# Token tiles side by side, the second attention's loads in order of use, and routing weights by powers of e on GpSimd

## The chip, the cores and the metric

The kernel runs on one core of one Trainium2 chip. The metric is the device time of one execution in microseconds (us), the median of several runs. The core has five engines that matter here: TensorE (PE in the profile) multiplies matrices, VectorE (DVE), ScalarE (ACT) and GpSimd (POOL) work on rows of 128 partitions, and SyncE (SP) does little but issue DMAs. Each runs its own list of instructions in order. SBUF is the memory on the core from which they work, PSUM the one that TensorE writes to.

## The reference, cut to what matters

The input is two images of 56 x 56 positions with 256 channels, all float32. Each image passes through a group norm and a neighbourhood attention ("Attention" below) with a residual. Then all 6272 positions, now called tokens, pass through two more layers:

```python
# x: (2, 256, 56, 56)
x = x + _L0_conv_ref(_gn(x), ...)        # 1x1 and 3x3 convolutions to q, k, v; 7x7 neighbourhoods,
                                         # dilation 1 and 2, softmax with a position bias; projection
t = _to_tokens(x)                        # (2, 3136, 256)
t = t + _L1_attn_ref(_ln_t(t), ...)      # linear attention, elu + 1, then a two-layer perceptron
t = t + _L1_ffn_ref(_ln_t(t), ...)       # 8 experts, two for each token
x = _from_tokens(t, x)

# inside _L1_ffn_ref
probs = softmax(xt @ Wr + br)
top_p, top_idx = top_k(probs, 2)
weights = top_p / top_p.sum(axis=-1, keepdims=True)
h = gelu(xe @ W1 + b1, approximate=False)     # for each expert: 256 -> 1024
y = h @ W2 + b2                               #                 1024 -> 256
out = sum over the two chosen experts of weights * y
```

The two weights of a token follow from its two largest logits m0 and m1 alone: with d = exp(m1 - m0) they are 1 / (1 + d) and d / (1 + d). That is what the kernel computes.

## The kernel before, in words

The program treats the first image's convolution and Attention, then the linear attention of the first image ("half 0"), then the second image's Attention, then the linear attention of the second image ("half 1"), and the experts wherever tokens are ready.

The linear attention works on groups of four tiles of 128 tokens, 14 groups in all. Groups 0 to 5 are in half 0, and groups 6 to 13 in half 1, of which the last three have two, two and one tile. The router's work for a group stands in `route`:

- `stats` and `norm` make normalised rows of the tokens, in a tile `row` whose columns hold the 256 channels, the token's number, the two weights and a flag.
- `top_two` finds the two largest logits and their experts, on VectorE.
- `weights` takes m1 - m0 (L2013), its Exp on ScalarE (L2014), and the two quotients on VectorE (L2015 to L2019; `rsum` is the first of these).
- `chosen` and `before` count, for each expert, the tokens up to here (L2056; `cnt` carries the count on to the next group). Two small matmuls (L2060, L2061) make places in the expert's list of them. VectorE turns those into integers `si`, through `sf` (L2063 to L2069).
- Eight indirect DMAs, issued by GpSimd, send the rows to their places in `xs` in DRAM. They are made by the helper `scatter` (L167), one for each of the four tiles and two experts.

A token's perceptron precedes this. Its matmuls are L1939 (with a Relu on ScalarE, L1942) and L1955, four blocks of which share three PSUM buffers (`ps_h`). VectorE frees each with `u` (L1962). The norm of the message takes squares on ScalarE (L1784) and a power of -1/2 on GpSimd (L260); `dt`, `z` and `qz` on VectorE (L1872, L1878, L1864) divide the linear attention by its denominator.

The experts work on tiles of 256 of an expert's tokens. For each, `fetch` issues on SyncE a DMA of the rows `xr` (L1521) and of the weights `w1e` and `w2e` (L1525, L1529); `turn` transposes the rows on TensorE (`px`, L1554), scales them to `xe` on VectorE and loads `b2e` (L1562). Then come the matmuls of L1585 with Gelu on ScalarE (L1589), those of L1603, the weighting on VectorE (L1609) and an indirect DMA that adds the result to the output (L167, `y`). The first 14 tiles run beside the second Attention and half 1; the rest, from tile 14 on, run alone afterwards. Beside the first of these the table for the last tiles is made from the final counts (matmul L1372, VectorE L1374), and `fill` pads the experts' lists.

Four things set the order of the work around the change.

- TensorE's order is written out by hand (`manual_schedule`, with strings of letters as turns). The other engines' instructions are placed by a scheduler that follows the order of the program, priorities (`high_priority`) and hints: `issue_after(x)` puts an instruction behind `x`.
- `newest` holds the last copy on VectorE ([0]) and the last power on GpSimd ([1]), to be named in such hints.
- Tiles of SBUF come from pools that open and close. A tile may lie over bytes of an older one, and its first writer then waits for the older one's last reader, even if that is a DMA. The pools of half 0 and half 1 have one-letter names: `sm` (small tiles, `p3s`) and `lp` (`p3l`) are two of them. `Tokens.place` lays out a half's tokens `t_00` to `t_05` (or `t_10` on) and, after them, their transposes `xT_00` to `xT_05`. The second Attention's pools open after half 0's close, so its first tiles lie over those.
- In the second Attention, `band0(r)` is the work of a band of eight image rows. Its tables of position bias are loaded by `fetch(s, r)` (L704, eight DMAs for one of s = 0), and the tokens' q and k by `prepare(g)` (`ld`, two DMAs, L789; transposed at L757). `v0` is loaded at L844. The scores are exponentiated (L647) and multiplied by the table (`p`, L648).

Of the kernel before, what the change touches and what calls it, by code (L numbers as in the profile page):

```python
# [13 lines left out]
F32 = mybir.dt.float32  # L14
AF = mybir.ActivationFunctionType
ALU = mybir.AluOpType
# [4 lines left out]
P = 128  # L21
# [24 lines left out]
E = 8  # L46
# [79 lines left out]
def hybrid_kernel(ctx: ExitStack, tc: tile.TileContext, a: dict, out: bass.AP):  # L126
# [5 lines left out]
    make_identity(nc, ident)  # L132
    mhalf = const.tile([P, 4], F32, name="mhalf")
    nc.vector.memset(mhalf, -0.5)


    td = dram.tile([B * T, C], F32, name="td")
# [20 lines left out]
    def apart(ins, mine, others, reason="rows of their own"):  # L158

        for group in others:  # L160
            tc.declare_no_dep(ins, group=group, reason=reason)
        for group in mine:
            tc.add_to_no_dep_group(group, ins)

    def scatter(dst, index, src, mine, others, **kw):

        ins = nc.gpsimd.indirect_dma_start(  # L167
            out=dst[:, :], out_offset=bass.IndirectOffsetOnAxis(ap=index, axis=0),
            in_=src, in_offset=None, **kw,
        )  # L170
        apart(ins.ins, mine, others)

    evac_n = [0]

    newest = [None, None]

    def evac(dst, src):

# [12 lines left out]
    class Tokens:  # L191
# [14 lines left out]
        def place(self, half, pool, late):  # L206

            pools = [pool] * (NH6 - 1) + [late]
            self.t[half] = [p.tile([P, 4, C], F32, name=f"t_{half}{i}", bufs=1) for i, p in enumerate(pools)]
            self.xT[half] = [  # L210
                p.tile([P, 2, 4 * P], F32, name=f"xT_{half}{i}", bufs=1) for i, p in enumerate(pools)
            ]

        def at(self, n0, n):

# [382 lines left out]
    class Attention:  # L598
# [115 lines left out]
        def run(self):  # L714
# [121 lines left out]
            def band0(r):  # L836
                yield blocks(8 * r + 16)
                if banks is not None and r == 0:
                    for k in range(2):
                        self.ahead[0, k] = self.fetch(0, k)  # L840
                yield from prepared(r + 1, 1)
                v0 = vp.tile([TT, 4, P], F32, name="v0")
                for c in range(4):
                    nc.sync.dma_start(  # L844
                        v0[:, c, :],
                        yimg[8 * r : 8 * r + 8, c * KC : (c + 1) * KC, 2 * C : 2 * C + P],
                    )
                i0, i1 = max(0, 8 * r - 3), min(HH, 8 * r + 11)
                ni = i1 - i0
                sums = [None]  # L850

                def chunk(hf, c):
                    j0, j1 = max(0, KC * c - 3), min(WW, KC * c + 17)
                    q = qT0[:, i0:i1, j0:j1]
                    got = []

                    def first():
                        got.append(self.scores(
                            TT, [(kT0[r][:, c].rearrange("p r c -> p (r c)"), q, 0)],
                            self.table(0, (r > 0) + (r == NG - 1), (c > 0) + (c == 3)), j1 - j0,  # L860
                        ))

                    def rest():
                        if c == 2 * hf:
                            po = self.ps_o.tile([P, 2, 512], F32, name="po")
                            sums[0] = po[:, :, : ni * 31].rearrange("p k (i j) -> p k i j", j=31)
                        h0 = (0, 25)[hf]
                        sub = sums[0][:, :, :, j0 - h0 : j1 - h0]
                        self.values(
                            TT, got[0], [(None, q, 0, v0[:, c, :], sub[:, 0], sub[:, 1])], c == 2 * hf  # L870
                        )

                    return first, rest

                def done(hf):
                    h0 = (0, 25)[hf]
                    for j, a0, a1 in ((r, i0, 8 * r + 4), (r + 1, 8 * r + 4, i1)):
                        o = 8 * j - 4
                        accumulate(
                            strip0(j)[:, :, a0 - o : a1 - o, h0 : h0 + 31], sums[0][:, :, a0 - i0 : a1 - i0, :]  # L880
                        )
                    if hf == 0:
                        return
                    for j in (r, r + 1) if r == NG - 1 else (r,):
                        a0, a1 = max(0, 8 * j - 4), min(HH, 8 * j + 4)
                        self.normalise(
                            strips0.pop(j)[:, :, a0 - 8 * j + 4 : a1 - 8 * j + 4, :].rearrange("p k r c -> p k (r c)"),
                            o0[:, a0:a1, :].rearrange("p r c -> p (r c)"), (a1 - a0) * WW,
                        )

                for hf in range(2):
                    for c in (2 * hf, 2 * hf + 1):
                        yield from step(*chunk(hf, c), (lambda hf=hf: done(hf)) if c % 2 else lambda: None)
# [731 lines left out]
    def linear(ph, tk, half, behind=None):  # L1625
# [286 lines left out]
        def feed_forward(n0, n, m2T, out):  # L1912
# [3 lines left out]
            for oc in range(4):  # L1916
                if oc == 0:
                    pa = ps_a.tile([P, 512], F32, name="pa", tag="a")
                    for ct in range(2):
                        for k in range(n):  # L1920
                            nc.tensor.matmul(
                                pa[32 * k : 32 * k + 32, :P], wr[:, ct, :], xT[:, ct, k * P : (k + 1) * P],
                                start=(ct == 0), stop=(ct == 1), skip_group_check=True,
                            )
                    la = lp.tile([P, P], F32, name="la", bufs=1)
                    evac(la[: 32 * n, :], pa[: 32 * n, :P])
                if oc == 2:
                    pl = ps_a.tile([P, 4, 32], F32, name="pl", tag="a")
                    nc.tensor.transpose(
                        pl.rearrange("p k e -> p (k e)")[:, : 32 * n], la[: 32 * n, :], ident[: 32 * n, : 32 * n]  # L1930
                    )
                    up = sm.tile([P, 4], F32, name="up1")[:, :n]
                    nc.vector.tensor_scalar(up, tk.up[:, n0 : n0 + n], 1.0, None, ALU.add)
                    lg = sm.tile([P, 4, E], F32, name="lg")
                    nc.vector.tensor_tensor(lg[:, :n], pl[:, :n, :E], bc(up, E), ALU.mult)
                p1 = ps_h.tile([P, 512], F32, name="p1", tag="h")
                for k in range(4):
                    rhs = xT[:, k, :] if k < 2 else m2T[:, k - 2, :w]
                    nc.tensor.matmul(  # L1939
                        p1[:, :w], fw1[:, k, oc * P : (oc + 1) * P], rhs, start=(k == 0), stop=(k == 3)  # L1940
                    )
                nc.scalar.activation(hT[:, oc, :w], p1[:, :w], AF.Relu, bias=hb[:, oc : oc + 1])  # L1942
                yield
# [66 lines left out]
        def weights(rt, ms, row, n):  # L2010

            r = rt.sm.tile([P, 4], F32, name="rsum")[:, :n]
            nc.vector.tensor_tensor(ms[1], ms[1], ms[0], ALU.subtract)  # L2013
            nc.scalar.activation(ms[1], ms[1], AF.Exp)  # L2014
            nc.vector.tensor_scalar(r, ms[1], 1.0, None, ALU.add)  # L2015
            nc.vector.reciprocal(r, r)
            nc.vector.tensor_tensor(row[:, :n, C + 1], ms[1], r, ALU.mult)
            nc.vector.tensor_scalar(ms[0], ms[1], -1.0, 1.0, ALU.mult, ALU.add)
            nc.vector.tensor_tensor(row[:, :n, C + 2], ms[0], r, ALU.mult)  # L2019

        def route(n0, n, logits):
# [32 lines left out]
            for k in range(n):  # L2054
                nxt = before[:, k + 1, :] if k < n - 1 else cnt
                nc.vector.tensor_tensor(nxt, before[:, k, :], m[:, k, :], ALU.add)  # L2056
            weights(rt, ms, row, n)
            yield
            pp = ns.bank()[:, : 4 * E].rearrange("p (k e) -> p k e", e=E)
            nc.tensor.matmul(pp[:, :n], rt.tri, m[:, :n], start=True, stop=False)  # L2060
# [4 lines left out]
            for k in range(K):  # L2065
                sf = sm.tile([P, 4], F32, name=f"sf{k}")[:, :n]
                nc.vector.tensor_tensor(ohs[k], ohs[k], slot, ALU.mult)
                nc.vector.tensor_reduce(sf, ohs[k], AX.X, ALU.add)
                nc.vector.tensor_copy(si[:, k, :n], sf)  # L2069
            store(n0, n)  # L2070
            late = [f"xlate{run}"] if (n0, n) in order[early1:] else []
            yield
            for k in range(n):
                with tc.issue_after(newest[1]) if late else nullcontext():
                    for kk in range(K):
                        scatter(
                            xs, si[:, kk, k : k + 1], row[:, k, :],
                            [f"xs{run}"] + late, [f"xs{run}"] + [f"xfull{run}"] * len(late),
                        )
                yield  # L2080
# [70 lines left out]
    def layer1(whole, tk, conv_ctx=None, conv=None, behind=None):  # L2151


        run = tk.run
        conv = conv or none

        def fill(n=1):
            for _ in range(n):
# [259 lines left out]
```

## Time and profile before

The three runs of the kernel before took 2051.68, 2052.05 and 2054.44 us.

| quantity | value |
|---|---|
| median of three runs | 2052.05 us |
| profiled execution | 2041.49 us |
| its span, first to last instruction | 2039.7 us |
| mean granted clock of TensorE | 0.962 |
| TensorE busy | 1843.3 us, 90% |
| VectorE busy | 1090.3 us, 53% |
| ScalarE busy | 698.6 us, 34% |
| GpSimd busy | 585.4 us, 29% |
| DMA, mean | 132 GB/s, 268.85 MB |

The profiled execution is one execution, 10.6 us shorter than the median. All durations below are from it. In the profile's rows an instruction is named by its line and engine, with output<-input by the program's names; "[17.93 <-DMA ld<-yd]" after a row says that the engine had stood idle for 17.93 us before it, and what ended that. A row of the waits gives engine and line, what it waited for, then the sum of us, the number of waits and the longest. "SPq" is the queue of SyncE. The clock is in shares of full speed.

### The profile page before, as it was taken

To read this page: it belongs to the slowest core of one execution; us is meant where nothing else is said; L and a number is where in the kernel's file an instruction comes from. 1 tells how busy PE (TensorE), PEld (TensorE's weight loads), DVE (VectorE), ACT (ScalarE), POOL (GpSimd) and SP (SyncE) were. 2 spreads that over 40 slices of the span, in tenths; PEclk is the share of its full clock that TensorE was granted. 3 is DMA by queue.
4 is the path that set the end of the run, shared out by engine and by line. 5 is a ranking of instruction groups with operands and counts; after the bars stand their busy time and mean duration, and the time that the engine had idled before them with its cause. 6 is when DMAs were issued, how large, how long until landed. Compare 5 with 4: busy or idle time off the path is not lost.

```text
span 2039.7 us, 27727 instructions
## 1 busy us (share of the span) xinstructions
PE 1843.3 (90%) x9996; PEld 1310.0 (64%) x9996; DVE 1090.3 (53%) x2741; ACT 698.6 (34%) x1321; POOL 585.4 (29%) x634
## 2 busy tenths in 40 slices
PE   6999898978899967899989989998699999999996
PEld 3545354556555644566668746566588888888885
DVE  6978988888887554565556335563232121222221
ACT  2333333334443313445436443223122222222332
POOL 4530230035012343111135201444323222323221
PEclk9999899989899987899999999999899999999998
DMA  4753332340111246663472210123368766676995
GB/s 110 158 135 116 122 110 54 109 143 17 40 42 50 79 115 201 156 166 106 138 226 81 57 52 24 57 80 98 89 199 243 194 188 196 189 208 189 287 287 160
DMA packets 200152, 268.85 MB, mean 132 GB/s; under 512 B 30952, under 2 KB 158614, under 8 KB 199760
## 3 DMA queue, kind: packets, MB, share of 16 engines
q1 hardware_dynamic: 167920, 223.95, 36.2%
q0 software_dynamic: 19728, 27.54, 7.4%
q10 hardware_dynamic: 12352, 15.43, 2.2%
q8 instruction: 83, 1.36, 0.3%
q14 instruction: 69, 0.57, 0.1%
HBM read 200.19 MB, written 70.95 MB: 133 GB/s over the span
## 4 chain that ended last, share of the span: by engine, by line
PE 45%; DMA 5%; DVE 4%; ACT 3%; POOL 1%; issue 1%; SPq 0%; ACTq 0%; DVEq 0%; POOLq 0%
PE ph L1585 13%; PE py L1603 13%; PE p L1939 3%; PE x L1603 2%; PE py L1955 2%; DMA y<-yt,idi 2%; PE x L1585 2%; PE po L657 2%; DMA xs<-in_c_fill 1%; PE kx L308 1%; PE kp L296 1%; PE s_ps L643 1%; PE px L1554 1%; PE x L348 1%; DMA xr<-xs 1%
## 5 line engine op out<-in xcount | busy, mean ns | idle before, releaser
L1585 PE MATMUL ph<-xe,w1e 128*128 128x256 f32 (+1 forms) x1448 | 312.6, 373 | 16.4 <-ACT hT L1589 9.8
L1603 PE MATMUL py<-w2e,hT 128*128 128x256 f32 x1392 | 311.4, 380 | 0.0
L1589 ACT ACTIVATE hT<-ph,sv 128x256 f32<-128x256 f32 (+1 forms) x362 | 166.0, 462 | 393.6 <-PE ph L1585 389.7
L1585 PEld LDWEIGHTS ph<-xe,w1e 128*128 128x128 f32 x1448 | 265.0, 193 | 55.8 <-ACT hT L1589 11.8
L1603 PEld LDWEIGHTS py<-w2e,hT 128*128 128x128 f32 x1392 | 260.8, 191 | 33.0
L167 POOL DMA_INDIRECT y<-yt,idi x101 | 160.3, 1587 | 315.4 <-DVE yt L1609 186.5
L570 DVE SCALAR_TENSOR_TENSOR yc<-ypad,w,yc 128x1120 f32<-128x1120 f32 x144 | 202.5, 1409 | 28.0 <-ACT yc L560 25.6
L260 POOL TENSOR_TENSOR rs<-rs,mhalf 128x2 f32<-128x2 f32 (+3 forms) x90 | 71.5, 798 | 315.9 <-DVE rs L259 285.4
L520 PE MATMUL py<-x_sb,wq 128*128 128x448 f32 (+1 forms) x384 | 152.7, 529 | 5.5 <-ACT ypad L526 3.9
L647 ACT ACTIVATE p<-s_ps 112x952 f32<-112x952 f32 (+5 forms) x88 | 102.1, 1160 | 146.2 <-PE s_ps L643 101.1
L648 DVE TENSOR_TENSOR p<-p,tab 112x952 f32<-112x952 f32 (+5 forms) x88 | 121.8, 1387 | 42.5 <-ACT p L647 41.8
L1537 DVE CAST idi<-xr 128x2 int32<-128x2 f32 (+1 forms) x53 | 11.3, 214 | 237.6 <-DMA xr<-xs 237.6
L1567 POOL TENSOR_SCALAR yt<-b2e,eq 128x256 f32<-128x256 f32 x101 | 51.1, 511 | 284.0 <-DMA b2e<-in_L_ffn_b 231.6
L541 PE MATMUL pc<-ypad,diag 128*128 128x448 f32 x324 | 131.5, 547 | 0.0
L1609 DVE SCALAR_TENSOR_TENSOR yt<-py,eq,yt 128x256 f32<-128x256 f32 x87 | 41.9, 482 | 165.9 <-PE py L1603 165.5
L167 POOL DMA_INDIRECT xs<-row,si x98 | 101.0, 1031 | 94.3 <-DVE si L2069 47.3
L520 PEld LDWEIGHTS py<-x_sb,wq 128*128 128x128 f32 x384 | 71.2, 196 | 67.1 <-issue 56.3
L563 DVE SCALAR_TENSOR_TENSOR yc<-ypad,w,yc 128x784 f32<-128x784 f32 x96 | 101.7, 1076 | 5.3 <-ACT yc L560 4.6
L657 PE MATMUL po<-p,v 98*32 98x170 f32 (+5 forms) x960 | 69.8, 372 | 33.8 <-issue 16.7
L1939 PE MATMUL p<-xT,fw 128*128 128x512 f32 (+1 forms) x208 | 95.9, 585 | 0.6 <-ACT hTl L1942 0.6
L1939 PE MATMUL p<-m2T,fw 128*128 128x512 f32 (+2 forms) x224 | 94.6, 545 | 0.0
L541 PEld LDWEIGHTS pc<-ypad,diag 128*128 128x128 f32 x324 | 60.0, 191 | 52.3 <-issue 48.8
(386 smaller groups left out, 2884.7 us busy)
## 6 DMA issues: line engine op xcount, KB each, us to landing
w1e<-in_L_ffn_W SPq DMA_DIRECT2D x53, 1024.0 KB
w2e<-in_L_ffn_W SPq DMA_DIRECT2D x53, 1024.0 KB
yd<-yc SPq DMA_DIRECT2D x24, 784.0 KB
ld<-yd SPq DMA_DIRECT2D x28, 448.0 KB
xr<-xs SPq DMA_DIRECT2D x48, 260.0 KB
b2e<-in_L_ffn_b SPq DMA_DIRECT2D x53, 128.0 KB
t<-td SPq DMA_DIRECT2D x12, 512.0 KB
y<-t ACTq DMA_DIRECT2D x24, 256.0 KB
```

Source lines behind the costliest of these rows:

```text
L167: ins = nc.gpsimd.indirect_dma_start(out=dst[:, :], out_offset=bass.IndirectOffsetOnAxis(ap=index, axis=0), in_=src, in_offset=None, **kw,)
L520: nc.tensor.matmul(py[:, :n, :], self.wq1[:, ct, oc * P : (oc + 1) * P], self.x_sb[:, ct, (q0 + g0) * WW : (q0 + g0 + n) * WW], start=(ct ...
L541: nc.tensor.matmul(pc, diag[:, tap, :], ypad[:, dy : dy + SHARE, dx : dx + WW], start=(tap == 0), stop=(tap == 8),)
L563: nc.vector.scalar_tensor_tensor(yc[:, y0:y1, :], src, w, yc[:, y0:y1, :], ALU.mult, ALU.add)
L570: nc.vector.scalar_tensor_tensor(yc[:, y0:y1, :], src, w, yc[:, y0:y1, :], ALU.mult, ALU.add)
L647: nc.scalar.activation(p[:nk, :, :n], s_ps[:nk, :, :n], AF.Exp)
L648: nc.vector.tensor_tensor(grid(p), grid(p), table[:nk], ALU.mult)
L657: nc.tensor.matmul(dst[hs] if w is None else den[hs], v[:nk, hs] if w is None else w[:nk, :], p[:, h, :, o : o + q.shape[2]], start=first ...
L1585: nc.tensor.matmul(p1, x.w1[:, ct, j * P : (j + 1) * P], x.xe[:, ct, :], start=(ct == 0), stop=(ct == 1),)
L1589: nc.scalar.activation(hT[:, j, :], p1, AF.Gelu, bias=x.sv[:, 4 + j : 5 + j])
L1603: nc.tensor.matmul(py, hT[:, j, h * P : (h + 1) * P], x.w2[:, j, :], start=(j == 0), stop=(j == NJ - 1),)
L1939: nc.tensor.matmul(p1[:, :w], fw1[:, k, oc * P : (oc + 1) * P], rhs, start=(k == 0), stop=(k == 3))
```

## The change

Four edits are made.

1. `Tokens.place` allocates the tiles of a half in turn, `t_i` then `xT_i`, where it allocated all `t` first and then all `xT`.
2. In `band0(0)` of the second Attention, the tokens of groups 0 and 1 (two `ld` each) are prepared together with tables (0, 0) and (0, 1), where both tables came first and then the tokens. In the built program SyncE's order is eight DMAs of a table, two `ld`, eight of a table, four `v0`, where it was sixteen of tables, two `ld`, `v0`. A third table, (1, 0), is fetched after `v0`.
3. `weights` takes `euler ** (m1 - m0)` on GpSimd, as one `pow` of 128 x n values, where it took Exp on ScalarE. The call of `weights` moves from before the matmuls L2060 and L2061 to after `si`. `newest[2]` is new: it is the last scatter issued, and the pow is put behind it by `issue_after`. It is reset to none at the start of `layer1`.
4. The logits' tile `lg` comes from pool `lp`, where it came from `sm`.

```diff
+    euler = const.tile([P, 4], F32, name="euler")
+    nc.vector.memset(euler, float(np.e))
...
         apart(ins.ins, mine, others)
+        return ins.ins
...
-    newest = [None, None]
+    newest = [None, None, None]
...
             pools = [pool] * (NH6 - 1) + [late]
-            self.t[half] = [p.tile([P, 4, C], F32, name=f"t_{half}{i}", bufs=1) for i, p in enumerate(pools)]
-            self.xT[half] = [
-                p.tile([P, 2, 4 * P], F32, name=f"xT_{half}{i}", bufs=1) for i, p in enumerate(pools)
-            ]
+            self.t[half], self.xT[half] = [], []
+            for i, p in enumerate(pools):
+                self.t[half].append(p.tile([P, 4, C], F32, name=f"t_{half}{i}", bufs=1))
+                self.xT[half].append(p.tile([P, 2, 4 * P], F32, name=f"xT_{half}{i}", bufs=1))
...
                 if banks is not None and r == 0:
                     for k in range(2):
+                        turning.extend(prepare(k))
                         self.ahead[0, k] = self.fetch(0, k)
+                    ready[0] = 2
                 yield from prepared(r + 1, 1)
...
+                if banks is not None and r == 0:
+                    self.ahead[1, 0] = self.fetch(1, 0)
...
-                    lg = sm.tile([P, 4, E], F32, name="lg")
+                    lg = lp.tile([P, 4, E], F32, name="lg")
...
             nc.vector.tensor_tensor(ms[1], ms[1], ms[0], ALU.subtract)
-            nc.scalar.activation(ms[1], ms[1], AF.Exp)
+            with tc.issue_after(newest[2]) if newest[2] else nullcontext():
+                nc.gpsimd.tensor_tensor(ms[1], euler[:, :n], ms[1], ALU.pow)
...
-            weights(rt, ms, row, n)
             yield
             pp = ns.bank()[:, : 4 * E].rearrange("p (k e) -> p k e", e=E)
...
                 nc.vector.tensor_copy(si[:, k, :n], sf)
+            weights(rt, ms, row, n)
             store(n0, n)
...
-                        scatter(
+                        newest[2] = scatter(
...
         conv = conv or none
+        newest[2] = None
```

## The prediction

> **What bounds the kernel now.** I read the page from its first parts down: which engine is busy, where it has holes, what it waits for there, and last the timelines of those stretches. The first fence is the page of the kernel before: busy time, and two rows of the 40 slices of 51 us.
>
> ```profile
> PE 1843.3 (90%) x9996; PEld 1310.0 (64%) x9996; DVE 1090.3 (53%) x2741; ACT 698.6 (34%) x1321; POOL 585.4 (29%) x634
> ...
> PE   6999898978899967899989989998699999999996
> ...
> PEclk9999899989899987899999999999899999999998
> ```
>
> TensorE (PE) is the bound at 90%, so only PE's holes can give or cost time. The two 6s in the middle are slice 14 (second attention begins, about 740 us) and slice 28 (experts alone begin, about 1460 us). The clock is low there too. The chain of waits agrees: 45% of the span PE, only 4% DVE, 1% POOL. Next the waits, PE's rows of the whole-run list, then SP's list for 1400 to 1480 us:
>
> ```profile
> PE x L757 <- DMA ld<-yd: 18.6, 2, 17.9
> PE px L1554 <- DMA xr<-xs: 16.8, 3, 14.2
> PE ph L1585 <- ACT hT L1589: 9.8, 3, 7.7
> ```
>
> ```profile
> SPq L1521 <- DMA xs<-row,si: 57.4, 1, 57.4
> ```
>
> Three single waits hold 39.8 us (17.9 + 14.2 + 7.7). The timelines say what ends each (SP, PE, ACT):
>
> ```profile
> 736.12 23.68 SPq L704 DMA_DIRECT2D tab<-fp  x16
> 759.91 0.96 SPq L789 DMA_DIRECT2D ld<-yd  x2
> ...
> 1468.87 0.34 SPq L1521 DMA_DIRECT2D xr<-xs  x1
> 1469.79 0.38 SPq L1525 DMA_DIRECT2D w1e<-in_L_ffn_W  x1
> ```
>
> ```profile
> 767.02 0.61 PE L757 MATMUL x<-ident,ld 112*128 112x112 f32 x2 [17.93 <-DMA ld<-yd]
> ...
> 1471.69 1.11 PE L1554 MATMUL px<-ident,xr 128*128 128x128 f32 x4 [14.15 <-DMA xr<-xs]
> 1475.42 6.70 PE L1585 MATMUL ph<-xe,w1e 128*128 128x256 f32 x16 [2.62 <-DMA w1e<-in_L_ffn_W]
> ```
>
> ```profile
> 1414.91 1.28 ACT L2014 ACT_TABLE_LOAD   x1
> 1421.76 0.20 ACT L2014 ACTIVATE m<-m 128x2 f32<-128x2 f32 x1 [5.57 <-DVE m L2013]
> 1421.98 1.28 ACT L1589 ACT_TABLE_LOAD   x1
> ```
>
> At 736 us SP issues 16 table loads for 23.68 us, and the `ld` that PE needs stands behind them. At 1410 to 1469 us SP stands 57.4 us at one `xr`. That transfer needs old rows of xs only, but its tile lies over the bytes of `si` and `sf`, which the last scatters read; `w1e`, `w2e` and `b2e` queue behind it. At 1415 us ACT holds Exp's place until DVE has the logits, and the Gelus that PE wants stand behind it.
>
> **What the Trainium skill says.** "ScalarE: Activation LUTs", What ACT_TABLE_LOAD costs: about 1283 ns; the trace agrees (1283 ns, 28 times at L1589, 3 times at L2014). "TensorE: Matmul & The Clock Gate", Architectural detail: ACT, DVE and GpSimd queues are strict FIFO, so a waiting instruction holds all behind it; the trace shows it (DVE L2030 at 1417.54 us stood 4.85 us for a row that POOL had queued behind five indirect DMAs). The same page, What's actually happening: an idle window of about 3.4 us halves PE's clock; the trace agrees (0.50 from 1462 to 1480 us, and 16 matmuls of L1585 took 6.70 us where 31 of them took 6.85 at 1524.80). "GPSIMD Engine Reference", When to use GPSIMD: its cores make the descriptors of software DMAs; the trace shows POOL busy 0.96 us or more and idle 0.30 between scatters.
>
> **The change part by part.** Signs: plus is slower. The instruction order of both built programs can be read without a run: PE's order is the same, ACT loses the Exps, POOL gains the pows, and SP and DVE are reordered.
>
> (a) Loads and token layout. With t and xT alternating, the first table's tile lies over tokens finished earlier, and SP's order becomes 8 tab, 2 `ld`, 8 tab, 4 v0, and so on: 16 tab, `ld` and `v0` are all still issued, in another order. `ld` can be issued at about 737 us (736.12 plus its place), and land by 742 to 744, since it took 767.02 − 759.91 = 7.1 us before. PE then starts its transposes when L1955 ends (749.09), but the next gate is the routing of group 5: L2060 ran at 771.36, and without the wait could run at about 765.2, after cnt on DVE (763.86). Alone: −6.2. It is eaten by (b).
>
> (b) Weights by powers on POOL. Removed: 14 Exps (0.205 us each on ACT). Added: 14 pows, priced by row L2036, the same operation at 128x4 (1.01 us), and one memset ahead of the span's work (nothing; all engines wait for loads there). But `issue_after(newest[2])` puts pow of group g behind the eight scatters of group g−1, and DVE's `rsum` of g, which waits for it, stands right behind the m2T copy of the next stage, ahead of dt, z, qz and u. So DVE stands for what is left of 8 × 1.27 = 10.2 us of scatters plus 1.0 us. On POOL itself nothing waits longer, since m − m, which pow reads, is done on DVE while the scatters run. A gain from (b) is excluded: nothing that PE waits for comes earlier by it. PE feels it when its fourth L1955 block waits for u (three PSUM buffers).
>
> First half. Groups 0 and 6 have no scatter ahead: nothing. Group 1: DVE free at about 659.9 (last scatter ends 659.4, less pow's overlap) instead of 650.6; u moves 662.77 → 669.4, PE +4.2. Groups 2, 3, 4, the same working with their shorter remainders: +2.9, +2.0, +1.8. Sum 10.9 at the end of L1955 (749.09 → 760.0). Group 5's DVE chain is 12.7 late, cnt 763.86 → 776.5, L2060 771.36 → 777.5: +6.1 to +6.4, since (a)'s slack takes the rest. Then scatters of group 4, pow of group 5 at about 790, `rsum` ahead of the second p·tab on DVE (780.90 → 791.9), si 785.1 → 795, last scatter 796.25 → 806, `xr` landed 800.42 → 810.2. `xr` gates PE's experts here (before: 5.79 us idle at 796.46 to 802.25). **First half +9.7**, bounds +6 and +13.
>
> Second half. Group 7: scatters 1278.10 to 1288.5, pow 1289.8, dt 1279.31 → 1290.6, u 1289.43 → 1295.2; PE's fourth block 1292.4 → 1295.65: +3.2. Group 8: 0, because u waits 5.5 to 8 us for ACT's squares anyway; that cover is ACT's, and it shrinks by only 0.2 us. Groups 9, 10, 11, 12: +3.1, +0.8, +0.9, 0. **Sum +8**, bounds +4 and +13.
>
> (c) Exp leaves ACT. Where Gelus and Exp alternate, both loads go: 6 × 1.283 us of ACT, and ACT no longer stands for DVE. The wait row gives what PE gets back: **−9.8**, the whole of PE ph <- ACT hT. What is late next there is PE itself, its own matmuls. Bounds −5 and −10.
>
> (d) `lg` to another pool. Together with (a)'s layout, the built allocation has `xr` of the first lone tile over a long finished token tile only; built SP order puts that `xr`, its `w1e`, `w2e`, `b2e` and the next `xr`, `w1e` ahead of the last scatters' wait. PE then goes on at 1457.5, xe at 1459.9, L1585 1460 to 1463.5. Next late is the count (L1372), which waits for DVE behind `rsum` of group 13, behind scatters of group 12 (1459.74 to 1464.6), pow 0.85, 0.7 on DVE: 1466.2. The second L1585 batch starts at 1466.65 instead of 1482.74: −16.1. Later `xr` come earlier too, so the 2.6 us left in the px row (16.8 − 14.2) go; I add 1.5 for a cold clock in the gap of 3.3. **−17.2**, bounds −8 and −19.
>
> Sum: 9.7 + 8 − 9.8 − 17.2 = **−9.3**. The profiled execution took 2041.49 us (span 2039.7 and 1.8 around it), so it would become 2032.2. The median of the runs shown is 2052.05, 10.6 above it; I take the difference over: **2042.7**. About 0.2%, 4.1 us, is what a measurement of this kernel can tell from no change.
>
> **The rivals.**
> 1. Slower: the DVE hold decides. One mechanism, pow behind eight scatters, at ten groups. Each hold is in full where DVE works just in time: 13 in the first half and 13 in the second, while ACT's gain is only 6 and the tail's 12 because DVE runs late into both: +8, 2060. It decides once PE's stalls exceed 9.8 + 17.2 = 27.0. For it: DVE waits 59.7 us for ACT at u already, so the u chain has little spare. Against: DVE is 53% busy, and in group 8 that wait covers all.
> 2. Tail hidden anyway, or (a) not doing what it says. If the count waits for scatters of group 13 too, the gain of (d) is 8: sum −0.1, 2052. If `ld` still comes 18 us after L1955, L2060 is 5 later: 2047.4. For it: SP's list shows one wait only, and a second may stand behind it. Against: the built order.
> 3. The hold is hidden: PE has enough queued. First half +4, second +3.5: −19.5, 2032.5.
>
> **How the numbers follow.** As worked, 2034 to 2048: 0.56. Rival 3, 2028 to 2034: 0.14. Rival 2, 2048 to 2056: 0.14. Rival 1, above 2056: 0.16. Faster is the first two, 0.70; within 0.2%, 0.14; slower, 0.16. The range 2030 to 2056 leaves out rival 1 and the low end of rival 3, 0.2 together.
>
> **What would show it.** Right: no `SPq L1521` wait of tens of us near 1410; px wait at 1457 gone, a short wait of L1372 for DVE near 1466 in its place; `ld` issued near 737; new DVE rows of rsum waiting for POOL, about 9 us at group 1 and 7; no L2014 table loads; `xr` about 10 us later at 800. Wrong: u not late at groups 1 and 7 (then faster), or PE's waits for DVE at L1955 and after above 27 us (then slower).

## The result, and the profile after

The changed kernel is faster. Its median is 2041.83 us over eight runs (2031.40 to 2044.09), that of the kernel before 2052.88 us over eight runs (2050.22 to 2058.74). The ratio is 0.9933, with a 95% interval of 0.9912 to 0.9953. That is 13.8 us less, between 9.6 and 18.1. Here and below the gain is taken from the ratio, which rests on all single executions; the two medians differ a little otherwise (11.1 us here). The prediction was 9.3 us less.

The profiled execution of the changed kernel took 2043.39 us, with a span of 2041.6. That is 1.9 us more than the profiled execution of before, although the medians say the opposite. Single executions of one kernel lay up to 13 us apart here. The first profile of before was a quick one, and the first of after a slow one. So both kernels were profiled again later, and stages are compared over three profiles of each. Lines of the changed kernel are some 2 to 8 higher than before (L757 is now L760, L1554 is L1561, L1372 is L1379, L1585 is L1592, L2060 is L2067).

The page of the changed kernel: busy time, and two rows of 40 slices of 51 us.

```profile
PE 1859.5 (91%) x9996; PEld 1317.3 (65%) x9996; DVE 1093.1 (54%) x2742; ACT 689.4 (34%) x1301; POOL 594.5 (29%) x648
...
PE   6999898978899895899999989999899999999996
...
PEclk9999899989899995899999989999999999999998
```

The 6 at slice 28 has become an 8: the hole before the lone experts is nearly closed. The one in the middle is still there, one slice later, as a 5 with a clock of 5. The next fence is the list of waits of the whole run of the changed kernel (engine, line, what it waited for: sum of us, number, longest).

```profile
DVE rsum L2023 <- POOL m L2022: 66.2, 11, 10.7
...
PE x L760 <- DVE qT L777: 10.8, 3, 10.4
```

The first row is new: VectorE stands 66.2 us, in eleven waits, for the power on GpSimd. (Two more at the same line, of 9.00 and 5.88 us, end with the power too, but the profile names no releaser for them.) The second is the hole in the middle. It is now a wait for VectorE, where before it was a wait for `ld`. The timelines of SP, and then of PE:

```profile
689.15 58.75 SPq L707 DMA_DIRECT2D tab<-fp  x8
748.02 0.96 SPq L792 DMA_DIRECT2D ld<-yd  x2
...
1434.10 0.35 SPq L1528 DMA_DIRECT2D xr<-xs  x1
1441.91 0.38 SPq L1532 DMA_DIRECT2D w1e<-in_L_ffn_W  x1
```

```profile
765.52 0.96 PE L760 MATMUL x<-ident,ld 112*128 112x112 f32 x8 [2.10 <-ACT sq L1791]
...
779.80 0.98 PE L760 MATMUL x<-ident,ld 112*128 112x112 f32 x4 [10.45 <-DVE qT L777]
780.58 0.50 PE L2067 MATMUL x<-chosen,tri 128*128 128x32 f32 x2
...
1472.52 0.63 PE L1561 MATMUL px<-ident,xr 128*128 128x128 f32 x4
1474.15 3.81 PE L1592 MATMUL ph<-xe,w1e 128*128 128x256 f32 x16 [1.00 <-DVE xe L1564]
...
1481.99 0.39 PE L1379 MATMUL pc<-cnt,ones 128*128 128x8 f32 x2 [3.90 <-DVE ce L1381]
```

`ld` is issued 12 us earlier (748.02, before 759.91) and no longer ends anything. L2067 stays late because group 5's routing on VectorE is late. At the end the lone tile's rows are there when PE asks: px follows without a wait, where it stood 14.15 us. The sixteen matmuls behind it take 3.81 us, not 6.70. The count comes 3.90 us late, behind the last power.

TensorE's order is the same in all kernels here, so the same matmul can be found in every trace. This table gives the time between such matmuls (us), named by their time in the first profile of before:

| stage | before, three profiles | after, three profiles | change of the means |
|---|---|---|---|
| 640 to 804 | 164.4, 173.0, 173.3 | 177.1, 175.5, 175.8 | +5.9 |
| 804 to 1036 | 231.9, 231.7, 234.4 | 231.3, 232.7, 226.4 | -2.5 |
| 1036 to 1195 | 158.8, 158.9, 158.4 | 161.2, 159.9, 161.6 | +2.2 |
| 1195 to 1412 | 218.1, 218.1, 216.7 | 222.1, 223.1, 223.7 | +5.3 |
| 1412 to 1426 | 12.6, 12.6, 12.6 | 3.7, 3.7, 3.7 | -8.9 |
| 1426 to 1457 | 31.4, 31.3, 32.5 | 33.9, 33.7, 33.8 | +2.1 |
| 1457 to 1485 | 27.8, 27.7, 27.2 | 13.4, 14.5, 14.6 | -13.4 |
| 1485 to 1545 | 60.1, 59.8, 61.0 | 62.5, 64.4, 59.2 | +1.7 |

### The profile page after: what moved, and what is told of

The parts are those of the page before. It is cut to its first block, busy times and chain, and to the rows that moved or that the text cites. A ratio compares the mean times of both kernels' runs of the same rounds, so it can differ in the third digit from the quotient of the medians.

```text
span 2041.6 us, 27719 instructions
## 1 busy us (share of the span) xinstructions
PE 1859.5 (91%) x9996; PEld 1317.3 (65%) x9996; DVE 1093.1 (54%) x2742; ACT 689.4 (34%) x1301; POOL 594.5 (29%) x648
## 4 chain that ended last, share of the span: by engine, by line
PE 43%; DMA 5%; DVE 5%; ACT 3%; POOL 2%; issue 2%; SPq 0%; ACTq 0%; DVEq 0%; POOLq 0%
PE ph L1592 12%; PE py L1610 12%; PE p L1946 3%; PE x L1610 2%; DMA y<-yt,idi 2%; PE x L1592 2%; PE py L1962 2%; PE po L660 2%; DMA xs<-in_c_fill 1%; PE x L351 1%; PE kx L311 1%; PE kp L299 1%; PE s_ps L646 1%; DMA xr<-xs 1%; POOL xs L169 1%
## 5 line engine op out<-in xcount | busy, mean ns | idle before, releaser
L1592 PE MATMUL ph<-xe,w1e 128*128 128x256 f32 (+1 forms) x1448 | 312.6, 372 | 10.2 <-DVE xe L1564 4.1
L1592 PEld LDWEIGHTS ph<-xe,w1e 128*128 128x128 f32 x1448 | 264.5, 192 | 50.1 <-DVE qz L246 6.0
L1962 PE MATMUL py<-fw,hTl 128*128 128x264 f32 x392 | 94.5, 398 | 10.5 <-DVE u L1969 10.5
L1962 PEld LDWEIGHTS py<-fw,hTl 128*128 128x128 f32 x392 | 76.2, 196 | 30.0 <-DVE u L1969 12.6
```

The lines of the kernel that those rows point to most:

```text
L1592: nc.tensor.matmul(p1, x.w1[:, ct, j * P : (j + 1) * P], x.xe[:, ct, :], start=(ct == 0), stop=(ct == 1),)
L1962: nc.tensor.matmul(py[:, : C + E], hT[:, kk, c0 : c0 + P], fw2[:, kk, :], start=(kk == 0), stop=(kk == 3),)
```

## The experiments

The experiments were run on three chips, and the kernel before was run again beside each batch. Its median was 2043.77 us on the first chip and 2053.90 and 2054.74 on the other two, so each version is compared with the kernel before on its own chip.

**The logits' tile alone.**

```diff
-                    lg = sm.tile([P, 4, E], F32, name="lg")
+                    lg = lp.tile([P, 4, E], F32, name="lg")
```

> The kernel before with one edit: the logits' tile comes from pool lp. In the built program this alone lets the first lone expert tile's rows lie over a finished token tile only, and SyncE issues them before the last scatters' wait. Theory (the tail is the gain): PE idle of 14.15 and 2.62 us at 1457 to 1475 us goes, about 3 us of waiting for the count come in place, so 12 to 17 us faster than before, about 2037 to 2040 us; no long wait of SyncE at the xr line near 1410 us. Rival (the tail was hidden behind the counts and last scatters): 0 to 4 us faster. Rival (the alternating token layout is what frees the rows): no change, and the 57 us wait stays.

Measured: 2028.08 us, where the kernel before, run beside it on the same chip, had 2043.77; ratio 0.9926 (0.9903 to 0.9949), 15.1 us faster. SP's and PE's timelines of this kernel:

```profile
1411.68 0.35 SPq L1521 DMA_DIRECT2D xr<-xs  x1
```

```profile
1459.39 0.63 PE L1554 MATMUL px<-ident,xr 128*128 128x128 f32 x4
1461.38 3.81 PE L1585 MATMUL ph<-xe,w1e 128*128 128x256 f32 x16 [1.35 <-DVE xe L1557]
...
1465.56 0.39 PE L1372 MATMUL pc<-cnt,ones 128*128 128x8 f32 x2 [0.26 <-DVE ce L1374]
```

An `xr` that was stuck to 1468.87 us now goes at 1411.68, and the stage from 1457 to 1485 takes 8.9 us, not 27.8. The count does not wait here (0.26): the 3.90 us in the changed kernel are the power's. So one small tile's place is the largest gain among the parts of the change. The rival that needed the token layout falls.

**The powers alone.**

```diff
-            nc.scalar.activation(ms[1], ms[1], AF.Exp)
+            with tc.issue_after(newest[2]) if newest[2] else nullcontext():
+                nc.gpsimd.tensor_tensor(ms[1], euler[:, :n], ms[1], ALU.pow)
...
-            weights(rt, ms, row, n)       # before the matmuls of L2060
+            weights(rt, ms, row, n)       # after si
```

> The kernel before with the powers on GpSimd alone: euler, newest[2], the moved call of weights. Theory (VectorE is held by pow behind eight scatters): about 12 us lost by the end of group 4, all of it carried on since the table loads and ld move back with it, some 15 us in the first half, 5 in the second, 8 to 10 won back where ScalarE no longer waits at 1415 us; 8 to 14 us slower than before, 2061 to 2067 us. Rival (the hold is covered by work that PE has queued): only ScalarE's gain is left, 5 to 10 us faster, 2043 to 2048 us.

Measured: 2056.63 us against 2043.77; ratio 1.0071 (1.0048 to 1.0094), 14.5 us slower. Its SP and PE:

```profile
746.79 25.63 SPq L707 DMA_DIRECT2D tab<-fp  x16
772.53 0.97 SPq L792 DMA_DIRECT2D ld<-yd  x2
```

```profile
779.74 0.60 PE L760 MATMUL x<-ident,ld 112*128 112x112 f32 x2 [19.03 <-DMA ld<-yd]
```

The delay of groups 1 to 4 moves the table loads and `ld` with it: `ld` is issued at 772.53, 12.6 us later than before, and PE still waits 19.03 us for it. The loss was expected at 8 to 14 us and came out a little above; the interval (9.8 to 19.2) holds that range's upper part. This part of the change is a loss by itself.

**Exp back on ScalarE.** The changed kernel, with the weights of before at their place of before (the reverse of the diff above).

> The changed kernel with the weights as before: Exp on ScalarE at its old place in the order; layout, order of loads and lg stay. Theory: the holds of VectorE go (20 us) and ScalarE's wait at 1415 us comes back (8 to 10 us), so 8 to 13 us faster than the changed kernel: 19 to 24 us faster than before, 2029 to 2034 us; with ld early, L2060 comes at about 765 us. Rival (the order of loads brings nothing, the routing of group 5 sets L2060): 14 to 17 us faster than before, level with the changed kernel or 3 to 5 faster. Rival (the powers are the gain of the change): slower than the changed kernel by 5 to 10 us.

Measured: 2020.83 us against 2043.77; ratio 0.9890 (0.9863 to 0.9918), 22.5 us faster than before. PE here:

```profile
761.44 1.01 PE L760 MATMUL x<-ident,ld 112*128 112x112 f32 x4 [11.87 <-ACT qT L769]
...
763.71 0.50 PE L2067 MATMUL x<-chosen,tri 128*128 128x32 f32 x2
```

With nothing holding VectorE, L2067 comes at 763.71 us. The idle time before it is 11.87 us of waiting for the copies of the transposes, which come after group 5's routing. The stage at 1412 to 1426 us is back at 12.3 us.

**Exp for groups of four tiles, the power for the last three.**

```diff
+            if n == 4:
+                nc.scalar.activation(ms[1], ms[1], AF.Exp)
+            else:
+                with tc.issue_after(newest[2]) if newest[2] else nullcontext():
+                    nc.gpsimd.tensor_tensor(ms[1], euler[:, :n], ms[1], ALU.pow)
...
-            weights(rt, ms, row, n)
+            if n < 4:                     # and for n == 4 at the place of before
+                weights(rt, ms, row, n)
```

> The changed kernel with Exp on ScalarE at its old place for the eleven groups of four tiles, and the power on GpSimd only for the last three groups of two, two and one tile, where ScalarE changes between Gelu and Exp. Theory: it keeps ScalarE's gain of 8 to 10 us at 1415 us and pays no hold of VectorE in the first half: 7 to 10 us faster than the kernel with Exp everywhere, 27 to 32 us faster than before, 2021 to 2026 us. Rival (the gain at 1415 us is turned into a wait for the power behind the scatters of the group before): within 3 us of the kernel with Exp everywhere.

Measured: 2013.04 us against 2043.77; ratio 0.9854 (0.9827 to 0.9880), 29.8 us faster than before. It is 7.8 us under the kernel above, on the same chip. The stage at 1412 to 1426 takes 3.7 us, that at 1457 to 1485 takes 13.6 (8.9 above): ScalarE's 8.6 us are won, and 4.7 of them go at the count, which waits 3.91 us for the last power, and at the slower matmuls behind it (5.39 us for sixteen, not 3.70).

**Both kernels once more.**

> The changed kernel once more, on the chip and at the time of the runs beside it, for a profile that can be set against the others stage by stage. Theory (the four parts add up: loads and layout -6, lg -15, powers +20, Exp -9): 8 to 14 us faster than before, and its idle time on TensorE as in the first profile, with less busy time between 430 and 1300 us. Rival (the first profile is typical and the gain small): within 4 us of before.

> The kernel before once more, for a second profile. Theory: the same idle times of TensorE at 749, 1416 and 1457 us (17.9, 7.7 and 14.2), and a span that differs from the first by how fast the matmuls between 92 and 1300 us ran. Rival (those waits come and go from run to run): idle times that differ by more than 2 us.

Measured: 2039.78 us (five runs) against 2053.90; ratio 0.9941 (0.9921 to 0.9961), 12.1 us faster. The profiled execution of after took 2044.96 us, the slowest of its five, and that of before 2049.43. The three waits of before were there again (17.6, 7.7 and 14.0 us). But its span was 8.0 us longer than in the first profile, and 8.6 of that lie in the one stage from 640 to 804 us, not spread from 92 to 1300 as I had expected. Where it comes from is told with the prediction's term (b).

**Loads and layout alone.** Edits 1 and 2 of the change, on the kernel before.

> The kernel before with the token layout and the order of loads alone. Theory: ld comes 12 to 17 us earlier, L2060 moves from 771.4 to about 765, set by the routing of group 5 on VectorE, and 4 to 8 us of it last to the end; the wait at the first lone tile stays at about 14 us: 5 to 8 us faster than before. Rival (the experts' rows gate the stretch up to 804 us and take it back): 0 to 3 us faster.

Measured: 2043.83 us against 2053.90; ratio 0.9957 (0.9946 to 0.9968), 8.8 us faster, between 6.6 and 11.1. L2060 ran at 766.35 us, and PE's wait at the first lone tile was 14.1 us as before. The loads are worth what was expected or a little more.

**All of the weights on GpSimd.** In the changed kernel, the lines after the power:

```diff
-            nc.vector.tensor_scalar(r, ms[1], 1.0, None, ALU.add)
-            nc.vector.reciprocal(r, r)
-            nc.vector.tensor_tensor(row[:, :n, C + 1], ms[1], r, ALU.mult)
-            nc.vector.tensor_scalar(ms[0], ms[1], -1.0, 1.0, ALU.mult, ALU.add)
-            nc.vector.tensor_tensor(row[:, :n, C + 2], ms[0], r, ALU.mult)
+            nc.gpsimd.tensor_scalar(r, ms[1], 1.0, 0.0, ALU.add, ALU.add)
+            nc.gpsimd.tensor_tensor(r, r, inv[:, :n], ALU.pow)      # inv holds -1
+            nc.gpsimd.tensor_tensor(row[:, :n, C + 1], ms[1], r, ALU.mult)
+            nc.gpsimd.tensor_scalar(ms[0], ms[1], -1.0, 1.0, ALU.mult, ALU.add)
+            nc.gpsimd.tensor_tensor(row[:, :n, C + 2], ms[0], r, ALU.mult)
```

> The changed kernel with the rest of the weights on GpSimd too: after the power, five short instructions (a sum, a power of -1, a difference, two products) in place of VectorE's five. The powers stand behind the scatters as in the changed kernel; only VectorE no longer waits for them. Theory (the cost is VectorE standing in its queue): the holds at groups 1 to 5 and 7 go, and the scatters of each group come 3 to 5 us later on GpSimd; 10 to 18 us faster than the changed kernel, 22 to 30 faster than before. Rival (the cost is GpSimd being late with the rows): no faster than the changed kernel, or up to 5 us slower.

Measured: 2024.24 us against 2053.90; ratio 0.9872 (0.9851 to 0.9892), 26.3 us faster than before and 14.2 more than the changed kernel on the same chip. The test keeps the power behind the eight scatters and even adds to GpSimd. VectorE around the power of group 1, first in the changed kernel and then in this one:

```profile
652.77 0.68 DVE L186 COPY m2T<-mts 128x512 f32<-128x512 f32 x1
662.39 0.17 DVE L2023 TENSOR_SCALAR rsum<-m 128x4 f32<-128x4 f32 x1 [8.93 <-POOL m L2022]
```

```profile
649.67 0.71 DVE L1881 STREAM_TRANSPOSE dt<-pd 128x512 f32<-128x512 f32 x1
...
659.30 0.43 DVE L1971 TENSOR_TENSOR u<-py,g 128x264 f32<-128x264 f32 x1 [1.41 <-ACT sq L1793]
```

GpSimd in the changed kernel, and in this one:

```profile
660.33 0.96 POOL L169 DMA_INDIRECT xs<-row,si  x1 [0.30 <-issue]
661.30 1.06 POOL L2022 TENSOR_TENSOR m<-euler,m 128x4 f32<-128x4 f32 x1
```

```profile
657.68 1.11 POOL L2024 TENSOR_TENSOR m<-euler,m 128x4 f32<-128x4 f32 x1
658.88 0.24 POOL L2025 TENSOR_SCALAR rsum<-m 128x4 f32<-128x4 f32 x1
...
659.27 1.02 POOL L2026 TENSOR_TENSOR rsum<-rsum,inv 128x4 f32<-128x4 f32 x1
```

In both, the power comes right after the last scatter. Where VectorE has nothing to do with it, `u` runs at 659.30 us, waiting for ScalarE alone; in the changed kernel it runs at 671.96. The cost is VectorE standing in its queue, and not the power or the late rows. The five instructions that left VectorE take 0.15 to 0.18 us each, under 1 us a group, so their own time is no rival to a hold of 8.93 us.

**The power ahead of the scatters, and a third pair.** The kernel with Exp for groups of four, without the hint:

```diff
-                with tc.issue_after(newest[2]) if newest[2] else nullcontext():
-                    nc.gpsimd.tensor_tensor(ms[1], euler[:, :n], ms[1], ALU.pow)
+                nc.gpsimd.tensor_tensor(ms[1], euler[:, :n], ms[1], ALU.pow)
```

> The kernel with Exp for the groups of four tiles and the power for the last three, without the hint that puts the power behind the scatters of the group before: in the built program each of the three powers stands ahead of those scatters on GpSimd. Theory: the wait of VectorE for the last power (5.9 us) and the wait of TensorE for the count (3.9 us) go, ScalarE's gain stays: 3 to 6 us faster than with the hint, 32 to 37 us faster than before. Rival (the scatters that now come after the power are late, and the rows of the second lone tile with them): level with the hinted kernel, 28 to 31 us faster than before.

> The changed kernel, a third profile beside one of before. Theory: stage by stage as in its first two profiles, first half 640 to 804 us 3 to 8 us longer than before, second half 4 to 6 longer, 9 shorter at 1412 to 1426 us, 13 to 14 shorter at 1457 to 1485 us, and a span 8 to 14 us under that of before. Rival (its profiled executions are slow as such): again a span within 5 us of before.

> The kernel before, a third profile. Theory: waits at 749, 1416 and 1457 us as in the first two; 640 to 804 us takes 164 to 173 us. Rival (first half really varies by over 10 us): outside that.

Measured: 2014.91 us against 2054.74; ratio 0.9808 (0.9785 to 0.9832), 39.5 us faster than before, where the changed kernel was 12 to 14 us faster. GpSimd and PE in it:

```profile
1445.63 0.55 POOL L2024 TENSOR_TENSOR m<-euler,m 128x1 f32<-128x1 f32 x1 [2.21 <-DVE m L2020]
...
1451.40 1.00 POOL L169 DMA_INDIRECT xs<-row,si  x1 [0.30 <-DVE si L2080]
```

```profile
1455.06 0.39 PE L1379 MATMUL pc<-cnt,ones 128*128 128x8 f32 x2 [0.26 <-issue]
```

The last power stands ahead of the scatters that start at 1451.40, and the count no longer waits. The gain over the hinted kernel was expected at 3 to 6 us. Whether there is any is open. Against before the two are 29.8 and 39.5 us faster, on two chips, with intervals that just touch; but their own medians are 2013.04 and 2014.91 us, and it is the kernel before that differs by 11 us. In their profiles the stage from 1457 to 1485 us is 4.7 us shorter without the hint (8.9, not 13.6), and the two beside it are 1.7 and 3.5 us longer (35.4 and 62.1, not 33.7 and 58.6). The wait of the count went as forecast; a gain from it is not shown.

The third pair took 2038.55 and 2051.47 us, 12.9 apart, as the medians say. In it 640 to 804 us took 175.8 us after and 173.3 before. That is 2.5 longer, where 3 to 8 had been expected. The second half was 7.0 longer (4 to 6 expected), and the two stages of the tail 8.8 and 12.6 shorter (9, and 13 to 14).

## Why the prediction was right, and where its terms were off

The sign, the time and the mechanism hold. By its steps:

**(a) Loads and layout**, -6.2 alone: 8.8 us alone (6.6 to 11.1). L2060 without holds was put at about 765.2 us and ran at 766.35 and, with `lg` as well, at 763.71. `ld` was put at about 737 us and came at 748.02, because the eight table loads ahead of it waited for stores of tokens to 748 (SyncE's waits for `y<-t` there were up to 27.1 us each); it was early enough all the same. What is late next was named rightly: group 5's routing.

**(b) The holds of VectorE.** The mechanism is shown by moving the waiting instructions to GpSimd. At group 1 the hold was 8.93 us, and it was put at 9. Counted from the start of the stage at 640 us, the end of L1955 came 11.4 us later in the first pair of profiles, where 10.9 had been worked out, and 7.4 and 7.7 in the other two. L2060 came 6.3 us later, where 6.1 to 6.4 had been worked out, and 2.5 and 2.8. **The term that was mis-sized is the first half's +9.7.** In the first pair it measured +12.7, but in the second and third +2.5 each. The changed kernel took much the same time in all three (175.5 to 177.1). The kernel before did not: all the working stood on its first profile, which was 9 us quicker from 640 to 804 us than the other two.

The traces show where those 9 us lie. ScalarE in the first profile of before, and then ScalarE and PE in the second (the third is like it):

```profile
743.79 0.38 ACT L1784 ACTIVATE sq<-py 128x256 bf16<-128x256 f32 x1 [1.09 <-PE py L1955]
...
779.96 0.90 ACT L647 ACTIVATE p<-s_ps 112x880 f32<-112x880 f32 x1 [1.25 <-PE s_ps L643]
```

```profile
748.10 0.38 ACT L1784 ACTIVATE sq<-py 128x256 bf16<-128x256 f32 x1 [5.81 <-PE py L1955]
...
788.87 0.90 ACT L647 ACTIVATE p<-s_ps 112x880 f32<-112x880 f32 x1 [5.28 <-remote]
```

```profile
741.40 5.50 PE L1955 MATMUL py<-fw,hTl 128*128 128x264 f32 x24
749.10 3.72 PE L1955 MATMUL py<-fw,hTl 128*128 128x264 f32 x8 [2.19 <-DVE u L1962]
...
790.25 0.60 PE L1372 MATMUL x<-cnt,ones 128*128 128x8 f32 x2 [4.23 <-ACT kT L769]
```

In the second profile ScalarE starts two instructions late. TensorE then stands 2.19 us for `u`, which needs the squares, and 4.23 us for a copy that stands behind L647 in ScalarE's queue. In the first profile TensorE has neither wait. What held ScalarE is open ("remote" is a releaser that the profile does not name). The kernel with the logits' tile alone, which differs here only in where the logits lie, took 164.0 us for this stage, so the quick form was no single case.

The other part is TensorE's clock. This is the whole stage in the first profile of before and in its second (window and its length, then busy us and count of PE, PEld, DVE, ACT and POOL, then PE's clock, DMA share and GB/s):

```profile
640.19:804.54 164.35, 133.32 (x622) 80.43 (x621) 96.06 (x419) 43.32 (x110) 70.67 (x73) 0.88 0.43 114
```

```profile
639.90:812.92 173.02, 138.16 (x623) 82.86 (x622) 96.56 (x419) 43.06 (x110) 70.28 (x73) 0.85 0.40 108
```

From the first to the second, the same matmuls are busy 4.8 us longer, at a lower clock, and the other 3.8 us are idle time. (In the changed kernel they are busy 140.21 us, at 0.84.) "TensorE: Matmul & The Clock Gate", What's actually happening, gives an idle window of about 3.4 us for a drop to half clock; here eight matmuls behind a wait of only 2.19 us took 3.72 us, where the 24 before them took 5.50. The prediction used such a drop for the tail and had no term for it here, where both kernels also idle over 10 us.

The rows `xr` at 800 us were forecast 10 us later. VectorE had them at 815.72 us, where it was 800.45 in the first profile of before and 808.76 in the second. But TensorE's wait there shrank from 5.79 to 1.47 us, so the rows alone did not set its time.

The second half's +8 measured +5.3 (the stage from 1195 to 1412). The tail's three powers cost another +2.1 at 1426 to 1457, which the working had at next to nothing.

**(c) Exp off ScalarE**, -9.8: the stage from 1412 to 1426 is 8.9 us shorter in all three pairs. In the timed runs, the same edit for three groups alone brought 7.8 us, the count's new wait included.

**(d) The logits' tile**, -17.2: alone 15.1 us (10.4 to 19.8). In the changed kernel the stage from 1457 to 1485 is 13.4 us shorter, against 16.1 worked out. The count's wait was foreseen at 3.3 us and was 3.90, its cause as named. The cold clock behind it, put at 1.5 us, shows as well: the sixteen matmuls after the count took 5.39 us, where they took 3.70 before. The 2.6 us that later rows should have given back went at first in the first pair (PE's wait of 2.27 us for `xr` at 1517 us is gone), but at 1541 us PE now waits 3.09 us for `xe` on VectorE, so nothing of it is left in the stage from 1485 to 1545.

The closeness of the sum is luck in part. In the means of the profiles the four terms come to -9.0 (+5.9, +7.4, -8.9 and -13.4), against -9.3: the first half lost 3.8 us less than worked out, and the tail gained 3.8 less. The stages without a term add some 4 us. Of these 3.4 lie before 640 us, where 0.8 follows the power of group 0 (put at nothing, since it has no scatter ahead) and the rest is open.

In the timed runs, alone, the parts give -15.1, -8.8 and +14.5, which is -9.4: just outside the interval of the whole in the first comparison (9.6 to 18.1 us faster), and inside that of the second (8.0 to 16.2). Rival 1, the hold deciding, had the right mechanism and too large a price. Rival 2 falls with the logits' tile alone (its 2047.4 us should read 2047.7 by its own sum). Rival 3's size for the first half (+4) is nearer to two of the three pairs than mine, but its reason is not the one: the hold is not hidden, since taking VectorE out of it brought 14.2 us.

What stays open: over the three pairs of profiles the stages come to about 5 us less, over the timed runs to 12 to 14. The pairs themselves differ by +1.9, -4.5 and -12.9 us. That is the scatter of single executions, and the traces don't tell in which stages the other executions gained.

## What to carry to other kernels

Here an instruction of 0.17 us that waited for another engine cost what stood behind it, and not what it computed. So before work is moved to an idle engine, ask where the reader of its result stands in its own queue, and either move the reader too or put the moved work ahead of long batches. When a load waits for something it has no data from, look at which tile's bytes its target lies over: moving a tile of 128 bytes per partition was worth 15.1 us here, the order of the loads 8.8. Size a loss of some 10 us from more than one profile of the stage, above all where TensorE idles and its clock is low.

## What the runs showed of the hardware that was not expected

Single executions of one kernel on one chip lay 12.7 us apart in the first comparison and 15.3 in one experiment (Exp back on ScalarE, 2011.86 to 2027.12), and the kernel before ran at 2043.77 us on one chip and at 2054.74 on another. A stage with long idle times came out at 164.4, 173.0 and 173.3 us in three executions of one kernel, where ScalarE started two instructions 4 to 5 us late in the longer two and TensorE's clock was lower. A wait of TensorE of 2.19 us was enough for half speed behind it. A power on GpSimd costs 1.04 us for 128x4 and 0.55 for 128x1, while a product or a sum of 128x4 there takes 0.19 to 0.24. The price of moving the rest of the weights there was thus some 2 us a group.
